# Input projections of an attention kernel, split into halves of the TensorE array's rows, with two-bank PSUM tiles

## Chip, cores and metric

One core of a Trainium2 chip runs the whole program. The metric is the device time of one execution in microseconds (us), the median of the runs shown. The profile is of one further execution on the same kernel.

The engines go by the profile's names: PE is TensorE, PEld its weight loads, DVE is VectorE, ACT is ScalarE, POOL is GpSimd, SP is SyncE, which issues most DMAs.

## What is computed

Two layers of multi-head attention with decomposed relative position biases, each on group-normalized input with a residual. There are 4 images of 32 x 32 positions (S = 1024) and 768 channels, 12 heads of 64 channels. Cut to what matters:

```
for layer in (0, 1):
    y = group_norm(x)                         # 32 groups
    q, k, v = y @ Wqkv (+ bias in layer 1)    # 12 heads, d = 64
    bias[h, w, kh, kw] = r_q . Rh[h - kh] + r_q . Rw[w - kw]
    scores = scale * q @ k.T + bias           # 1024 x 1024 for each head
    out = softmax(scores) @ v
    x = x + out @ Wproj + bproj
# layer 0: scale = 1/8, r_q = q.   layer 1: q is scaled twice, r_q = q / 8
```

All data are fp32.

## The kernel before

**Units of work.** A layer and an image together are one of 8 stages, called images 0 to 7 below. An image has 6 pairs of heads (`NP`), a pair has 8 blocks of 128 queries (`NT`). The main loop (from L517) runs over 48 x 8 = 384 units. In unit n of pair g it does, in this order on PE:

- what earlier units left over in the list `early`: position products (`positions`, 16 small matmul records on a tile `tp`) and loads
- the scores of the following unit (`scores`, L328): for two heads and two halves of the keys, 4 fp32 matmuls. Head 0 uses rows 0 to 63 of the array, head 1 rows 64 to 127, and they write different PSUM tiles
- a share of the projections (`take`): the input projections of the next pair (`project_in`, L222: q, k and v, two halves of 512 columns each, so 6 groups of 6 fp32 matmuls), then output projections of this or the last image (`project_out`, groups of 3 matmuls)
- in every second unit `weigh`: the product with the values for two blocks, 16 matmuls on halves of the array's columns (tile `av`)
- twice in a pair `turn_values`: transposes of v on PE (tile `vt`).

An fp32 matmul shows as two MATMUL records and two LDWEIGHTS records. In most pairs units 0 to 5 each hold one whole input group (q, q, k, k, v, v) and units 6 and 7 two output groups each. Pair 5 of an image takes output groups in units 0 and 1 first and the input groups in units 2 to 7. Pair 4 also carries the normalization of the next image (`norm`): its small matmuls `gm` and `gb` stand behind the first four input groups. In image 0 and at the end of image 7, where fewer output groups are there, groups reach across units.

**What the other engines do in a unit.** DVE makes the negated scores with their row minimum (L342, one instruction for each head), ACT the exponentials (L346), DVE the reciprocals (L350), POOL the weights (L353), DVE the 32 x 32 block transposes (L367). The weights then go through DRAM and come back as `pt`, four units later used by `weigh`. POOL also lays out the biases `sc` two units ahead (L323).

**PSUM.** [...]`ps_s` has 3 buffers of two banks, used by the scores and by `tp`. `ps_m` has 2 buffers of one bank, used by everything else on PE: `pj` (input projection), `o`, `av`, `vt`, `gm`, `gb`. A group on a `ps_m` buffer can start when the group before the last one has been evicted.

**Evictions of the input projections.** q goes through ACT with its scale (L247, L249), k and v through DVE (L251, L253). v is written in a strided order. When a q half is there, `positions` for it is put into `later` (or `early` for the first pair of an image) and so runs two (one) units later; `scores` of the next pair needs both halves of q and k; `turn_values` needs v.

**What sets the order.** PE runs in the program's order (a manual schedule). The other engines' instructions are put in an order by the compiler's scheduler, which then stands; each engine works through its own queue in that order. `early`, `later` and `late` are lists of steps for the next unit, for the one after it, and for the end of a unit.

The core of the two steps that the change touches:

```
            nc.tensor.matmul(
                t, lhsT=w[:, c, :], rhs=xn[c][:, cols],
                start=(c == 0), stop=(c == NC - 1),
            )
...
                nc.tensor.matmul(
                    ps[h][:, cols], lhsT=q[rows, n * P : (n + 1) * P], rhs=k[rows, cols],
                    start=True, stop=True,
                )
```

The first is the input projection, over all 128 rows. The second is the scores, where `rows` is one half.

Of the kernel before, what the change touches and what calls it, by code (L numbers as in the profile page):

```python
# [30 lines left out]
P = 128  # L32
# [16 lines left out]
def attention_blocks(ctx: ExitStack, tc: tile.TileContext, a: dict, out: bass.AP):  # L49
# [20 lines left out]
    ps_s = ctx.enter_context(tc.tile_pool(name="ps_s", bufs=3, space=PSUM))  # L70
# [74 lines left out]
    nc.gpsimd.tensor_scalar(bqkv[:, 0, :], bqkv[:, 0, :], SCALE * SCALE, None, ALU.mult)  # L145
# [22 lines left out]
    def group_mean(cols, name):  # L168
        t = ps_m.tile([P, HALF], FP, tag="m", name=f"gm_{name}")
        for c in range(NC):  # L170
            nc.tensor.matmul(
                t[0:NG, 0:1], lhsT=grp[:, c, :], rhs=cols(c), start=(c == 0), stop=(c == NC - 1)
            )
        return t[0:NG, 0:1]

    def to_channels(g, name):
        t = ps_m.tile([P, HALF], FP, tag="m", name=f"gb_{name}")
        for c in range(NC):
            nc.tensor.matmul(
                t[:, c : c + 1], lhsT=grpT[:, c * P : (c + 1) * P], rhs=g, start=True, stop=True  # L180
            )
        return t[:, 0:NC]
# [39 lines left out]
    def project_in(g, which, i):  # L222
# [11 lines left out]
        t = ps_m.tile([P, HALF], FP, tag="m", name=f"pj_{g}_{which}_{i}")  # L234
        for c in range(NC):
            nc.tensor.matmul(  # L236
                t, lhsT=w[:, c, :], rhs=xn[c][:, cols],
                start=(c == 0), stop=(c == NC - 1),
            )
            if c < NC - 1:  # L240
                yield True
        if which == 2:
            t = t.rearrange("p (y k j) -> p y k j", y=2, k=NT)
        bias = bqkv[:, which, pair : pair + 1]
        if which == 0:
            if l == 0:
                nc.scalar.activation(to, t, AF.Copy, scale=SCALE)  # L247
            else:
                nc.scalar.activation(to, t, AF.Identity, bias=bias, scale=SCALE * SCALE)  # L249
        elif l == 0:  # L250
            nc.vector.tensor_copy(to, t)  # L251
        else:
            nc.vector.tensor_scalar(to, t, bias, None, ALU.add)  # L253
        if which == 0:
            (later if pair else early).append(lambda: positions(g, i))
        if which == 2 and i == 1:
            late.extend([lambda: turn_values(g, 0), lambda: turn_values(g, 1)])
# [6 lines left out]
    def turn_values(g, i):  # L264


        if i == 0:
            v_of[g] = vpool.tile([P, NT, P], FP, tag="v", name=f"v_{g}")
        t = ps_m.tile([P, 4, P], FP, tag="m", name=f"vt_{g}_{i}")
        for j in range(4):  # L270
            at = 4 * i + j
            nc.tensor.transpose(t[:, j, :], qkv_of[g, 2][:, at * P : (at + 1) * P], ident)  # L272
        nc.scalar.copy(v_of[g][:, 4 * i : 4 * i + 4, :], t)  # L273

    def positions(g, i):
# [6 lines left out]
        ps = ps_s.tile([P, 2, 4, P], FP, tag="s", name=f"tp_{g}_{i}")  # L282
# [45 lines left out]
    def scores(g, n):  # L328
        q, k = qkv_of[g, 0], qkv_of[g, 1]
        ps = [ps_s.tile([P, S], FP, tag="s", name=f"s_{g}_{n}_{h}") for h in range(2)]  # L330
        for i in range(2):
            cols = slice(i * HALF, (i + 1) * HALF)
            for h in range(2):
                rows = slice(h * D, (h + 1) * D)
                nc.tensor.matmul(  # L335
                    ps[h][:, cols], lhsT=q[rows, n * P : (n + 1) * P], rhs=k[rows, cols],
                    start=True, stop=True,
                )
        st = small.tile([P, 3, 2], FP, tag="sm", name=f"sm_{g}_{n}")
        for h in range(2):  # L340
            sc = sc_of[g, n, h].rearrange("p y x -> p (y x)")
            nc.vector.tensor_tensor_reduce(  # L342
                out=sc, in0=ps[h], in1=sc, scale=-1.0, scalar=BIG, op0=ALU.add, op1=ALU.min,
# [37 lines left out]
    def weigh(g, quarter):  # L381
        if quarter == 0:
            attn_of[g] = apool.tile([P, S], FP, tag="attn", name=f"attn_{g}")
        av = ps_m.tile([P, HALF], FP, tag="m", name=f"av_{g}_{quarter}")[:, : 2 * P]
# [45 lines left out]
    def project_out(im, p, o, i):  # L430
# [7 lines left out]
        t = ps_m.tile([P, HALF], FP, tag="m", name=f"o_{im}_{p}_{o}_{i}")  # L438
# [168 lines left out]
```

## Time and profile before

| | us |
|---|---|
| median of 3 runs | 3851.63 (3844.91 to 3860.61) |
| profiled execution, its own time | 3855.63 |
| its span, first to last instruction | 3853.9 |
| PE busy | 3716.4 (96%) |
| DVE busy | 2353.1 (61%) |
| POOL busy | 2316.3 (60%) |
| ACT busy | 1148.9 (30%) |
| granted TensorE clock, mean | 0.987 |

Busy times add up the durations of an engine's instructions where they do not overlap. A row of the costliest groups gives line, engine, operation, what it writes and reads, its count, then busy time and the mean ns of one, then the idle time of the engine just before and what ended it. In the timeline each row has start and duration in us, and in brackets the idle time of that engine before it.

### The profile page before, as it was taken

What the parts mean: (1) busy time and instruction counts of PE and PEld (TensorE: products, weight loads), DVE (VectorE), ACT (ScalarE), POOL (GpSimd) and SP (SyncE); (2) the same over time, 40 slices, a digit from 0 to 9 for tenths busy, and PEclk for the clock granted to TensorE, in tenths of its full rate; (3) what the DMA queues carried; (4) which work ended last, traced back from release to release, by engine and by line L of the source; (5) the groups of instructions that cost most, each with busy time, mean ns of one, the idle gap of its engine ahead of it and who ended that gap; (6) DMA issues with size and microseconds to landing.
All of it is one profiled execution on the core that took longest, in us unless ns stands there. A gap on an engine that the chain in (4) does not pass through costs nothing.

```text
span 3853.9 us, 45565 instructions
## 1 busy us (share of the span) xinstructions
PE 3716.4 (96%) x16128; PEld 1716.4 (45%) x16128; DVE 2353.1 (61%) x3520; ACT 1148.9 (30%) x1848; POOL 2316.3 (60%) x1555
## 2 busy tenths in 40 slices
PE   8899999999999999999999999999999999999998
PEld 3444444444444444444444444444444444444443
DVE  4566656656566665665656656666566665656663
ACT  1233232222332323333323332233323332233330
POOL 4666556655565656666566655666566665666671
PEclk9999999999999999999999999999999999999999
DMA  5778778887788887887878888888788887988877
GB/s 179 266 274 302 276 272 294 295 291 277 279 293 283 307 289 264 305 301 277 312 254 298 292 279 295 289 298 297 255 318 290 291 278 278 314 284 282 293 271 269
DMA packets 620820, 1094.73 MB, mean 284 GB/s; under 512 B 235056, under 2 KB 295728, under 8 KB 571440
## 3 DMA queue, kind: packets, MB, share of 16 engines
q1 hardware_dynamic: 569904, 1041.49, 77.9%
q10 hardware_dynamic: 50688, 50.34, 3.8%
q8 instruction: 127, 2.08, 0.2%
q14 instruction: 101, 0.83, 0.1%
HBM read 588.36 MB, written 503.32 MB: 283 GB/s over the span
## 4 chain that ended last, share of the span: by engine, by line
PE 77%; DMA 8%; DVE 5%; ACT 3%; issue 3%; POOL 2%; SPq 1%; DVEq 0%; ACTq 0%; POOLq 0%
PE pj L236 32%; PE av L388 16%; PE s L335 15%; PE o L440 11%; PE tp L287 2%; ACT sc L346 2%; DVE tb L367 2%; DMA tdr<-t 2%; POOL sc L353 2%; DVE sc L342 1%; SPq L313 1%; DMA xs<-in_x 1%; DMA td<-tb 1%; PE vt L272 1%; DMA w<-in_wqkv 1%
## 5 line engine op out<-in xcount | busy, mean ns | idle before, releaser
L323 POOL TENSOR_TENSOR sc<-rel 128x1024 f32<-128x1024 f32 x768 | 1456.3, 1916 | 270.3 <-DMA rel<-tdr 140.9
L236 PE MATMUL pj<-xn,w 128*128 128x512 f32 x3456 | 1579.0, 606 | 31.5 <-DVE k L251 12.7
L353 POOL TENSOR_SCALAR sc<-sc,sm 128x1024 f32<-128x1024 f32 x768 | 854.9, 1126 | 1205.0 <-DVE sm L350 1200.1
L346 ACT ACTIVATE sc<-sc,sm 128x1024 f32<-128x1024 f32 x768 | 878.5, 1144 | 1863.7 <-DVE sm L342 1793.1
L367 DVE STREAM_TRANSPOSE tb<-sc 128x1024 f32<-128x1024 f32 x768 | 921.0, 1227 | 464.9 <-POOL sc L353 462.6
L342 DVE CUSTOM_DVE_ANT_0 sc<-s,sc 128x1024 f32<-128x1024 f32 x768 | 906.1, 1216 | 303.3 <-PE s L335 303.2
L236 PEld LDWEIGHTS pj<-xn,w 128*128 128x128 f32 x3456 | 638.4, 191 | 951.1 <-issue 884.0
L388 PE MATMUL av<-pt,v 128*64 128x256 f32 x6144 | 730.6, 392 | 61.3 <-DVE g L202 22.9
L335 PE MATMUL s<-k,q 64*128 64x512 f32 x3072 | 764.1, 610 | 4.1 <-DVE sm L342 4.0
L388 PEld LDWEIGHTS av<-pt,v 128*64 128x64 f32 x6144 | 435.8, 141 | 406.9 <-issue 72.4
L440 PE MATMUL o<-attn,wo 128*128 128x512 f32 x1152 | 524.4, 605 | 5.0 <-DVE res L449 4.2
L335 PEld LDWEIGHTS s<-k,q 64*128 64x128 f32 x3072 | 268.2, 186 | 318.5 <-issue 306.4
L440 PEld LDWEIGHTS o<-attn,wo 128*128 128x128 f32 x1152 | 211.5, 190 | 310.4 <-issue 291.2
L350 DVE RECIPROCAL sm<-sm 128x2 f32<-128x2 f32 x384 | 63.6, 166 | 442.1 <-ACT sc L346 442.1
L292 ACT COPY t<-tp 128x1024 f32<-128x1024 f32 x96 | 97.1, 1011 | 292.9 <-PE tp L287 291.2
L393 DVE COPY attn<-av 128x256 f32<-128x256 f32 x192 | 78.5, 409 | 120.5 <-PE av L388 120.0
L273 ACT COPY v<-vt 128x512 f32<-128x512 f32 x96 | 56.1, 585 | 319.3 <-PE vt L272 319.1
L346 ACT ACTIVATION_READ_ACCUMULATOR sc<-sc,sm 128x1 f32 x768 | 143.1, 186 | 0.0
L287 PE MATMUL tp<-tab,q 64*128 64x128 f32 x1536 | 111.6, 285 | 6.6 <-ACT q L249 3.1
L287 PEld LDWEIGHTS tp<-tab,q 64*128 64x128 f32 x1536 | 93.2, 187 | 52.9 <-issue 32.7
L447 DVE SCALAR_TENSOR_TENSOR res<-o,bo,res 128x512 f32<-128x512 f32 x96 | 70.1, 730 | 16.5 <-PE o L440 15.0
L449 DVE TENSOR_TENSOR res<-o,res 128x512 f32<-128x512 f32 x96 | 64.6, 674 | 22.3 <-PE o L440 12.3
(47 smaller groups left out, 646.1 us busy)
## 6 DMA issues: line engine op xcount, KB each, us to landing
td<-tb SPq DMA_DIRECT2D x384, 1024.0 KB, 5.9
pt<-td SPq DMA_DIRECT2D x384, 1024.0 KB, 7.4
w<-in_wqkv SPq DMA_DIRECT2D x144, 384.0 KB, 7.5
tdr<-t ACTq DMA_DIRECT2D x96, 512.0 KB, 6.8
rel<-tdr SPq DMA_DIRECT2D x768, 32.0 KB, 2.0
part<-res SPq DMA_DIRECT2D x96, 256.0 KB, 6.5
res<-part SPq DMA_DIRECT2D x96, 256.0 KB, 4.6
wo<-in_wo SPq DMA_DIRECT2D x84, 192.0 KB, 6.0
```

Of the source, the lines that this page charges most:

```text
L236: nc.tensor.matmul(t, lhsT=w[:, c, :], rhs=xn[c][:, cols], start=(c == 0), stop=(c == NC - 1),)
L287: nc.tensor.matmul(ps[:, h, j, :], lhsT=q[rows, at * P : (at + 1) * P], rhs=tabs[l][rows, :], start=True, stop=True,)
L292: nc.scalar.copy(t, ps.rearrange("p h j r -> p j h r"))
L323: nc.gpsimd.tensor_tensor(sc, rel[:, h, 0, n, :].unsqueeze(2).to_broadcast([P, HW, HW]), rel[:, h, 1, n, :].unsqueeze(1).to_broadcast([P, ...
L335: nc.tensor.matmul(ps[h][:, cols], lhsT=q[rows, n * P : (n + 1) * P], rhs=k[rows, cols], start=True, stop=True,)
L342: nc.vector.tensor_tensor_reduce(out=sc, in0=ps[h], in1=sc, scale=-1.0, scalar=BIG, op0=ALU.add, op1=ALU.min, accum_out=st[:, 0, h : h + 1],)
L346: nc.scalar.activation(sc, sc, AF.Exp, bias=st[:, 0, h : h + 1], scale=-1.0, accum_out=st[:, 1, h : h + 1],)
L353: nc.gpsimd.tensor_scalar(sc, sc, st[:, 2, h : h + 1], 1.0, ALU.mult, ALU.mult)
L367: nc.vector.transpose(tb[:, :, j, :], sc_of[g, n, h])
L388: nc.tensor.matmul(av[rows, :], lhsT=v_of[g][:, k, rows], rhs=pt_of[g, quarter, h][:, :, k, :], start=(k == 0), stop=(k == NT - 1),)
L393: nc.vector.tensor_copy(attn_of[g][:, at : at + 2 * P].rearrange("p (n r i) -> p r n i", n=2, r=4), av.rearrange("p (r n i) -> p r n i", n ...
L440: nc.tensor.matmul(t, lhsT=w[:, c - c0, :], rhs=attn_of[im * NP + c][:, cols], start=(c == c0), stop=(c == c1 - 1),)
```

## The change

```
-    ps_s = ctx.enter_context(tc.tile_pool(name="ps_s", bufs=3, space=PSUM))
+    ps_s = ctx.enter_context(tc.tile_pool(name="ps_s", bufs=2, space=PSUM))
     ps_m = ctx.enter_context(tc.tile_pool(name="ps_m", bufs=2, space=PSUM))
...
-    nc.gpsimd.tensor_scalar(bqkv[:, 0, :], bqkv[:, 0, :], SCALE * SCALE, None, ALU.mult)
...
-        t = ps_m.tile([P, HALF], FP, tag="m", name=f"pj_{g}_{which}_{i}")
+        t = ps_m.tile([P, 2, HALF], FP, tag="m", name=f"pj_{g}_{which}_{i}")
         for c in range(NC):
-            nc.tensor.matmul(
-                t, lhsT=w[:, c, :], rhs=xn[c][:, cols],
-                start=(c == 0), stop=(c == NC - 1),
-            )
+            for a in range(2):
+                rows = slice(a * D, (a + 1) * D)
+                nc.tensor.matmul(
+                    t[:, a, :], lhsT=w[rows, c, :], rhs=xn[c][rows, cols],
+                    start=(c == 0), stop=(c == NC - 1),
+                )
             if c < NC - 1:
                 yield True
+        t = [t[:, a, :] for a in range(2)]
         if which == 2:
-            t = t.rearrange("p (y k j) -> p y k j", y=2, k=NT)
-        bias = bqkv[:, which, pair : pair + 1]
-        if which == 0:
-            if l == 0:
-                nc.scalar.activation(to, t, AF.Copy, scale=SCALE)
-            else:
-                nc.scalar.activation(to, t, AF.Identity, bias=bias, scale=SCALE * SCALE)
-        elif l == 0:
-            nc.vector.tensor_copy(to, t)
+            t = [x.rearrange("p (y k j) -> p y k j", y=2, k=NT) for x in t]
+        if l == 0:
+            nc.scalar.copy(to, t[0])
         else:
-            nc.vector.tensor_scalar(to, t, bias, None, ALU.add)
+            nc.scalar.activation(to, t[0], AF.Identity, bias=bqkv[:, which, pair : pair + 1])
+        nc.vector.tensor_tensor(to, t[1], to, ALU.add)
...
-            late.extend([lambda: turn_values(g, 0), lambda: turn_values(g, 1)])
+            late.append(lambda: turn_values(g))
...
+    def turn_values(g):
+        v_of[g] = vpool.tile([P, NT, P], FP, tag="v", name=f"v_{g}")
+        t = ps_m.tile([P, NT, P], FP, tag="m", name=f"vt_{g}")
+        for k in range(NT):
+            nc.tensor.transpose(t[:, k, :], qkv_of[g, 2][:, k * P : (k + 1) * P], ident)
+        nc.scalar.copy(v_of[g], t)
...
-        ps = ps_s.tile([P, 2, 4, P], FP, tag="s", name=f"tp_{g}_{i}")
+        ps = ps_m.tile([P, 2, 4, P], FP, tag="m", name=f"tp_{g}_{i}")
...
+        scale = SCALE if g // NP < B else SCALE * SCALE
...
-                out=sc, in0=ps[h], in1=sc, scale=-1.0, scalar=BIG, op0=ALU.add, op1=ALU.min,
+                out=sc, in0=ps[h], in1=sc, scale=-scale, scalar=BIG, op0=ALU.add, op1=ALU.min,
```

Each fp32 matmul of an input projection becomes two, one for channels 0 to 63 of a chunk and one for 64 to 127. They write two banks of one tile. ACT copies the first bank to SBUF (with the bias in layer 1) and DVE then adds the second bank to it, for q, k and v alike. The scale of q moves into the scale of L342. All tiles of `ps_m` now have two banks, still in 2 buffers; `ps_s` goes from 3 buffers to 2, and `tp` moves from `ps_s` to `ps_m`. `turn_values` runs once in a pair over 8 blocks, in place of twice over 4, with one copy of 1024 elements in place of two of 512.

More of the change, by code (lines that the diff above doesn't have):

```diff
@@ L168, in group_mean @@
     def group_mean(cols, name):
-        t = ps_m.tile([P, HALF], FP, tag="m", name=f"gm_{name}")
+        t = ps_m.tile([P, S], FP, tag="m", name=f"gm_{name}")
         for c in range(NC):
@@ L176, in to_channels @@
     def to_channels(g, name):
-        t = ps_m.tile([P, HALF], FP, tag="m", name=f"gb_{name}")
+        t = ps_m.tile([P, S], FP, tag="m", name=f"gb_{name}")
         for c in range(NC):
@@ L262, in project_in @@
         yield True
[L264 to L273, printed above, removed]
+    def turn_values(g):
[4 more added lines that the diff above has]
+        nc.scalar.copy(v_of[g], t)
     def positions(g, i):
@@ L383, in weigh @@
             attn_of[g] = apool.tile([P, S], FP, tag="attn", name=f"attn_{g}")
-        av = ps_m.tile([P, HALF], FP, tag="m", name=f"av_{g}_{quarter}")[:, : 2 * P]
+        av = ps_m.tile([P, S], FP, tag="m", name=f"av_{g}_{quarter}")[:, : 2 * P]
         for k in range(NT):
@@ L437, in project_out @@
         w, res = wo_of[im, p, o], res_of[im, p, o, i]
-        t = ps_m.tile([P, HALF], FP, tag="m", name=f"o_{im}_{p}_{o}_{i}")
+        t = ps_m.tile([P, S], FP, tag="m", name=f"o_{im}_{p}_{o}_{i}")[:, :HALF]
         for c in range(c0, c1):
```

## Prediction

> **What bounds the kernel now.** I read the busy times, then the costliest groups, then the timeline of two units (numbers 2 and 3 of a pair) and the table of windows for whole pairs.
>
> ```profile
> PE 3716.4 (96%) x16128; PEld 1716.4 (45%) x16128; DVE 2353.1 (61%) x3520; ACT 1148.9 (30%) x1848; POOL 2316.3 (60%) x1555
> ...
> L236 PE MATMUL pj<-xn,w 128*128 128x512 f32 x3456 | 1579.0, 606 | 31.5 <-DVE k L251 12.7
> L335 PE MATMUL s<-k,q 64*128 64x512 f32 x3072 | 764.1, 610 | 4.1 <-DVE sm L342 4.0
> L449 DVE TENSOR_TENSOR res<-o,res 128x512 f32<-128x512 f32 x96 | 64.6, 674 | 22.3 <-PE o L440 12.3
> ```
>
> PE is the bound. The second and third row say more: 3456 full-array records take 1579 us, 457 ns for each; 3072 half-array records of the same 512 columns take 764, so 497 for each two. Two halves run side by side. The fourth row is an add from PSUM and SBUF as the change makes.
>
> ```profile
> 1050.00 1.89 PE L335 MATMUL s<-k,q 64*128 64x512 f32 x8
> 1051.81 0.30 PEld L236 LDWEIGHTS pj<-xn,w 128*128 128x128 f32 x2 [0.76 <-issue]
> 1051.91 1.23 DVE L342 CUSTOM_DVE_ANT_0 sc<-s,sc 128x1024 f32<-128x1024 f32 x1 [2.34 <-PE s L335]
> 1052.35 0.19 PEld L236 LDWEIGHTS pj<-xn,w 128*128 128x128 f32 x1 [0.24 <-issue]
> 1052.78 0.19 PEld L236 LDWEIGHTS pj<-xn,w 128*128 128x128 f32 x1 [0.24 <-issue]
> 1057.08 2.37 DVE L367 STREAM_TRANSPOSE tb<-sc 128x1024 f32<-128x1024 f32 x2 [1.25 <-POOL sc L353]
> 1057.16 0.30 PEld L335 LDWEIGHTS s<-k,q 64*128 64x128 f32 x4 [0.76 <-issue]
> 1059.08 0.30 PEld L236 LDWEIGHTS pj<-xn,w 128*128 128x128 f32 x2 [0.76 <-issue]
> 1059.38 0.65 DVE L251 COPY k<-pj 128x512 f32<-128x512 f32 x1
> 1059.95 1.21 DVE L342 CUSTOM_DVE_ANT_0 sc<-s,sc 128x1024 f32<-128x1024 f32 x1
> ```
>
> Inside a group a weight load comes every 0.43 us (1052.35, 1052.78), so 12 records should take 5.15 us; from 1051.81 to 1057.16 they take 5.35. The next scores, 4 pairs or 1.72, take 1.92 (1057.16 to 1059.08). Each passage between full and half array costs 0.20 us: the weight load comes 0.76 after the last one, in place of 0.24, because it isn't laid under the matmuls before. From `tp` to the scores, both on halves, the trace shows no such time (2 to 3 ns over the plain spacing).
>
> ```profile
> 2107.00:2182.30 75.30, 75.30 (x329) 34.58 (x329) 48.85 (x75) 23.62 (x38) 48.02 (x32) 1.00 0.86 294
> 2257.60:2347.30 89.70, 84.11 (x386) 40.31 (x385) 55.61 (x82) 26.47 (x41) 48.95 (x33) 0.98 0.79 283
> 2347.30:2423.80 76.50, 72.22 (x319) 32.82 (x318) 46.74 (x71) 23.02 (x37) 46.47 (x32) 1.00 0.88 300
> ```
>
> The first row is an ordinary pair (pair 2 of image 4): PE never stops in 75.3 us. The next are pairs 4 and 5: 5.6 and 4.3 us of PE waiting.
>
> [...]a k eviction whose matmuls ended at 1057.2 started at 1059.38, behind two transposes.
>
> **The change part by part.** The sum is made against the profiled execution (3855.63 us, 4.0 above the median).
>
> *Matmuls.* 1728 fp32 matmuls become 1728 pairs. By the scores' spacing (429 ns for a pair of records, 429 for a full record) their time is unchanged. The two halves of the scores already write two banks; that accumulating over six chunks costs nothing more is shown by `av`, whose pairs accumulate eight times at 216 ns for 256 columns. I take 0.
>
> *Passages.* In the order of the matmuls I count 292 from scores to `pj`, 90 from `pj` to scores, 35 from `pj` to `tp`. All become half to half: 417 x 0.20 = **83 us less**, or 9 x 0.20 = 1.8 in an ordinary pair. `pj` to `av` remains a change of form; one transpose step fewer saves 8 more passages to `tp`, 1.6, which I leave aside.
>
> *Eviction.* ACT takes 0.6 (row q<-pj, 595 ns in layer 0), then DVE adds, 0.67 for q and k; for v, strided, its copy took 1.07 and I take 1.1, bounds 0.67 and 1.6. ACT (30%) has long done its exponentials when a group ends, so its copy hides. DVE gets 96 additional instructions (q), 64 us, and the k and v ones change little. What counts is when a `ps_m` buffer comes free. From the timeline, with 0 at a unit's first L342: second transpose ends at 7.5 (1059.45 - 1051.91); a group ends at 5.3; the add is ready at 6.0, when the first transpose is on DVE. The second is then ready too and stands first in the program, as for k above, so the add runs to 8.15. q's buffer used to be free at 5.9.
>
> *Who waits for that.*
> (a) Ordinary pair: k's first half (unit 2) now takes the buffer of q's second half, since `tp` stands between on the other. Unit 1 has no `av`: with the passage gone its group starts 0.2 ahead of the L342 that is my 0, so PE is back after 5.15 + `tp` 0.9 + scores 1.72 - 0.2 = 7.6; the buffer comes at 8.15, and the signal and a weight load that is not laid under anything add some 0.2: 0.7 us. There are 27 such pairs (0 to 3 of images 1 to 6, 0 to 2 of image 7): **+19**.
> (b) Pair 4, 7 times. After q's first half and `gm`, `av` needs q's buffer. Before, it started at 2271.44, 5.7 after the first L342 of its unit (2265.77); the add ends at 8.2: +2.6. After q's second half and `gb`, `tp` needs that buffer: it started 6.7 after (2283.73 against 2277.06), now at 8.3: +1.5. DVE catches up in these stalls, so about 1.0 of its lag at the next scores goes. 3.1 x 7 = **+22**.
> (c) Pair 5, 7 times: `tp` follows q's second half at once and needs its data. It waited 0.9 before; now until 8.2 in place of 6.1: 2.1 x 7 = **+15**.
> (d) Seven pairs with few output groups (0 to 3 of image 0, 3 to 5 of image 7) follow DVE's chain more than PE: two units are there 2 x 1.72 + 9 x 0.86 + `av` 3.5 = 14.7 on PE, and 2 x 7.5 + evictions on DVE. Their 1.8 isn't harvested, and q adds 2 x 0.6: 3.1 x 7 = **+22**.
>
> *Other edits at nothing.* Two score buffers in place of three: scores need both L342 of the unit before, done 2.4 after it starts, while PE is back after 7 or 10.5; DVE would have to lag by 4 us. `vt` in one piece: one copy of 1.0 in place of two of 0.59, hidden under the next scores. The scale on POOL ran once. No DMA is added; `tp`'s store waits for the same copy, in pair 5 some 2 us later, well ahead of its use a pair on.
>
> *Sum.* -83 + 19 + 22 + 15 + 22 = -5: 3851 in the profile, **3847 us** on the median's footing. v's add at 1.6 or 0.67 adds up to 15 or takes 10.
>
> **The rivals.**
> *The adds slip in between the two transposes.* For it: output evictions do so in unit 6 (a residual add starts at 1084.73 between transposes at 1083.56 and 1085.30). Against it: k doesn't, with an earlier ready time. The buffer is then free 1.15 sooner: (a) vanishes, (b) and (c) lose about 3.5 of 5.2 a stage (24 us). 3847 - 19 - 24 = **3804**.
> *Slower: DVE's queue behind one buffer.* In (a) the next unit's first L342 (1.2 us) stands ahead of q's add on DVE, so k waits 1.9 in place of 0.7. For it: DVE is already 0.8 late after a unit without `av` (L342 at 1059.95, scores ended at 1059.15), and unit 1 now has such an eviction too. Against it: by the dependences the add is ready a scores' length earlier. 34 pairs x 1.2 = 41: **3888**. It decides from 1.8 us of waits in a pair, where the passages' gain is used up.
> *The halves don't run side by side*, so the change doesn't do what it says: 1728 x 0.86 = 1486 more, 5330. The score rows speak against it.
>
> **How the numbers follow.** A measurement of this kernel can tell some 0.5%, 19 us, from no change. Forecast (within 19 us) 0.46; gain kept 0.27; slower by the queue 0.25; not side by side 0.02. Range: from the first rival less some microseconds of a cheaper v add, 3800, to the second, 3888, and a little of the dearer v add: 3892. 0.46 lies within 3830 to 3866.
>
> **What would show it.** Right: the weight load of `pj` after scores comes 0.24, not 0.76, after the last one; `pj` pairs every 0.43; an ordinary pair lasts 74.2; in its unit 2 `pj` waits for DVE q some 0.7; pair 4 grows by 1 or 2 us; PE's idle time names DVE q at `av` and `tp`. Wrong: ordinary pairs at 73.5 (first rival), at 75.5 or more (second), or 0.86 between pairs of records (third).

## The result, and the profile after

| | before | after |
|---|---|---|
| median of the runs side by side | 3848.4 us (3844.9 to 3860.6, 4 runs) | 4035.9 us (4029.6 to 4042.8, 4 runs) |
| ratio | 1 | 1.0482, 95% interval 1.045 to 1.0513 |
| span of the profiled execution | 3853.9 us | 4030.2 us |
| granted TensorE clock, mean | 0.987 | 0.962 |

The changed kernel is 4.8% slower; 3847 with a range of 3800 to 3892 had been forecast. On the page of the changed kernel, the busy times and four of the costliest groups, and below them the last of these rows as it was before:

```profile
PE 3696.3 (92%) x19584; PEld 1778.8 (44%) x19584; DVE 2397.5 (59%) x3616; ACT 1314.8 (33%) x1992; POOL 2307.3 (57%) x1554
...
L241 PE MATMUL pj<-xn,w 64*128 64x512 f32 x6912 | 1555.0, 595 | 46.3 <-DVE q L254 37.7
...
L387 PE MATMUL av<-pt,v 128*64 128x256 f32 x6144 | 734.0, 393 | 81.1 <-DVE v L254 31.8
L333 PE MATMUL s<-k,q 64*128 64x512 f32 x3072 | 778.2, 620 | 9.6 <-DVE sm L341 9.5
...
L439 PE MATMUL o<-attn,wo 128*128 128x512 f32 x1152 | 540.2, 619 | 74.6 <-DVE v L254 69.4
```

```profile
L440 PE MATMUL o<-attn,wo 128*128 128x512 f32 x1152 | 524.4, 605 | 5.0 <-DVE res L449 4.2
```

PE's busy time fell by 20 us while the span grew by 176: PE does not work longer, it waits. 6912 half-array records take 1555 us where 3456 full ones took 1579, so the halves do run side by side. The last column says who waits: before, the output rows waited 5.0 us in all; now they wait 69 us for DVE's add of v (L254), and `av` another 32. Those rows are not the ones that the change rewrote.

Two units of an ordinary pair in the timeline of the changed kernel (some of the PE, PEld and DVE lines of pair 2 of image 4, units 1 and 2):

```profile
2243.04 5.32 PE L241 MATMUL pj<-xn,w 64*128 64x512 f32 x24
2243.24 1.22 DVE L341 CUSTOM_DVE_ANT_0 sc<-s,sc 128x1024 f32<-128x1024 f32 x1 [0.81 <-PE s L333]
2243.47 0.19 PEld L241 LDWEIGHTS pj<-xn,w 64*128 64x128 f32 x2 [0.24 <-issue]
2248.41 2.37 DVE L366 STREAM_TRANSPOSE tb<-sc 128x1024 f32<-128x1024 f32 x2 [1.25 <-POOL sc L352]
2249.08 1.89 PE L333 MATMUL s<-k,q 64*128 64x512 f32 x8
2250.70 0.65 DVE L254 TENSOR_TENSOR q<-pj,q 128x512 f32<-128x512 f32 x1
2251.41 0.30 PEld L241 LDWEIGHTS pj<-xn,w 64*128 64x128 f32 x4 [1.27 <-DVE q L254]
2251.41 1.13 PE L241 MATMUL pj<-xn,w 64*128 64x512 f32 x4 [0.44 <-DVE q L254]
```

The weight loads of `pj` come 0.24 us after the load before, with no 0.76 at the passage, and 24 records take 5.15 us to `tp` (2243.04 to 2248.19, the start of the `tp` records). The q add stands behind both transposes and ends 8.1 after the unit's first L341, and k's first half starts after it: 0.60 us later than the matmul spacing allows. This part went as forecast.

The windows of pairs 2, 4 and 5 of image 4 in the changed kernel (columns: start and end, length, then busy time and instructions of PE, PEld, DVE, ACT, POOL; then PE's clock, DMA share, GB/s):

```profile
2225.30:2299.86 74.56, 73.89 (x401) 35.48 (x401) 49.69 (x76) 27.45 (x41) 47.74 (x32) 1.00 0.88 300
2374.10:2474.95 100.85, 84.27 (x450) 41.06 (x449) 55.43 (x84) 30.04 (x44) 47.94 (x32) 0.92 0.71 252
2474.95:2551.60 76.65, 73.33 (x382) 34.67 (x384) 47.95 (x72) 24.91 (x39) 46.60 (x32) 1.00 0.86 301
```

The first is the ordinary pair: 74.6, of which 0.3 is a wait elsewhere; the pairs next to it take 74.28 and 74.27. Pair 5: 76.7 against 76.5. Pair 4: 100.9 against 89.7, with PE's clock at 0.92. Where it is lost is seen in the DVE timeline of that pair (three more normalizations, L215, at the dots):

```profile
2448.81 2.37 DVE L366 STREAM_TRANSPOSE tb<-sc 128x1024 f32<-128x1024 f32 x2 [1.25 <-POOL sc L352]
2457.56 0.81 DVE L215 TENSOR_SCALAR xn<-xn,mean,rstd 128x1024 f32<-128x1024 f32 x1 [6.38 <-DMA xn<-mid]
...
2462.11 1.05 DVE L254 TENSOR_TENSOR v<-pj,v 128x512 f32<-128x512 f32 x1
2463.06 0.81 DVE L215 TENSOR_SCALAR xn<-xn,mean,rstd 128x1024 f32<-128x1024 f32 x1
2463.79 1.22 DVE L341 CUSTOM_DVE_ANT_0 sc<-s,sc 128x1024 f32<-128x1024 f32 x1
```

and in PE's timeline beside it:

```profile
2448.60 1.88 PE L333 MATMUL s<-k,q 64*128 64x512 f32 x8
2450.41 2.84 PE L439 MATMUL o<-attn,wo 128*128 128x512 f32 x6
2463.21 5.17 PE L439 MATMUL o<-attn,wo 128*128 128x512 f32 x6 [9.96 <-DVE v L254]
2468.31 3.67 PE L387 MATMUL av<-pt,v 128*64 128x256 f32 x32
```

The matmuls of the v group ended at 2448.6. Its add is queued on DVE behind four normalizations of the next image's input, which wait for their load until 2457.56; DVE stands idle for 6.4 us with the v add and the score reductions (L341) behind it. The reductions come some 13.3 us after their scores ended (2463.79 against 2450.5). In the kernel before, the v eviction and the reductions stood first:

```profile
2330.92 1.10 DVE L253 TENSOR_SCALAR v<-pj,bqkv 128x512 f32<-128x512 f32 x1
2331.88 1.20 DVE L342 CUSTOM_DVE_ANT_0 sc<-s,sc 128x1024 f32<-128x1024 f32 x1
...
2336.24 0.81 DVE L212 TENSOR_SCALAR xn<-xn,mean,rstd 128x1024 f32<-128x1024 f32 x1 [2.00 <-DMA xn<-mid]
```

In the seven pairs 4 together PE is idle for 115.0 us, for 44.6 before. 69.4 of it are the waits of `o` for v's add; at the same place `av` waited 19.9 for output evictions before.

The second thing to see is 5.17 against 2.84 us for the same six records: after the stall PE starts a record every 0.853 us instead of every 0.429, with a granted clock of 0.53 (2463.2 to 2468.3).

By part of the run, as differences of the profiled spans (start: until the first L341; pairs: from one pair's first score reduction to the next). The second column spreads the prediction's terms over the same parts, with the passages that each holds in the order of the matmuls: 9 in an ordinary pair, 7 in pair 4, 8 in pair 5, 66 in image 0 and the end. (Its terms add up to -6.4 with their decimals, -5 as the prediction rounds them.)

```
part                                   forecast   after - before, us
start                                    -0.4        +26.2
image 0, pairs 0 to 3                    +3.6        +43.7
image 7, pairs 3 and 4                   +1.8        +33.3
pair 4, seven times                     +11.9        +60.3
pair 5, seven times                      +3.5        +10.7
images 1 and 2, pairs 1 to 3             -6.6        +18.5
images 3 to 7, ordinary pairs, 14       -15.4        -14.7
pair 0 and the tail                      -4.8         -1.7
sum                                      -6.4       +176.2
```

The compiler leaves a fixed order of DVE's queue in each kernel. Below are its start and its part in pair 4, read from the traces of the kernels before and after and of three experiments. First line of each: evictions (q, k, v) and statistics of a loaded half of a later image (.) ahead of the first score reduction. Second line: pair 4 around the normalizations (tb transpose, sc reduction, xn normalization, v its eviction or add, res output eviction, rcp reciprocal; small steps left out).

```
before                .....kkv.v.
                      tb tb v sc sc xn res rcp xn tb res tb xn
layout alone          .....kkv.v.
                      tb tb v sc sc xn res rcp xn tb res tb xn
full rows, two steps  q...q...kkv.v.
                      tb tb v sc sc xn res rcp xn tb res tb xn
halves, one step      .........k.k...v...v
                      sc sc rcp tb tb xn xn xn v xn xn sc sc xn res
after                 ..q....q...k.k...v...v
                      sc sc rcp tb tb xn xn xn xn v xn sc sc xn res
```

### The profile page after: what moved, and what is told of

It reads as the page before. It is cut to its first block, busy times and chain, and to the rows that moved or that the text cites. A ratio compares the mean times of both kernels' runs of the same rounds, so it can differ in the third digit from the quotient of the medians.

```text
span 4030.2 us, 52794 instructions
## 1 busy us (share of the span) xinstructions
PE 3696.3 (92%) x19584; PEld 1778.8 (44%) x19584; DVE 2397.5 (59%) x3616; ACT 1314.8 (33%) x1992; POOL 2307.3 (57%) x1554
## 4 chain that ended last, share of the span: by engine, by line
PE 58%; DVE 11%; DMA 9%; ACT 8%; issue 7%; POOL 4%; SPq 1%; ACTq 0%; DVEq 0%; POOLq 0%
PE pj L241 19%; PE av L387 14%; PE s L333 12%; PE o L439 9%; ACT sc L345 8%; DVE tb L366 4%; POOL sc L352 4%; DMA xs<-in_x 3%; DVE sc L341 2%; PE tp L285 2%; DMA tdr<-t 2%; PE vt L270 1%; SPq L311 1%; DMA xn<-mid 1%; DVE q L254 1%
## 5 line engine op out<-in xcount | busy, mean ns | idle before, releaser
L241 PE MATMUL pj<-xn,w 64*128 64x512 f32 x6912 | 1555.0, 595 | 46.3 <-DVE q L254 37.7
L341 DVE CUSTOM_DVE_ANT_0 sc<-s,sc 128x1024 f32<-128x1024 f32 x768 | 907.3, 1216 | 365.4 <-PE s L333 365.3
L241 PEld LDWEIGHTS pj<-xn,w 64*128 64x128 f32 x6912 | 672.8, 189 | 891.5 <-issue 780.9
L333 PE MATMUL s<-k,q 64*128 64x512 f32 x3072 | 778.2, 620 | 9.6 <-DVE sm L341 9.5
L439 PE MATMUL o<-attn,wo 128*128 128x512 f32 x1152 | 540.2, 619 | 74.6 <-DVE v L254 69.4
L333 PEld LDWEIGHTS s<-k,q 64*128 64x128 f32 x3072 | 283.9, 192 | 330.9 <-issue 298.3
L285 PEld LDWEIGHTS tp<-tab,q 64*128 64x128 f32 x1536 | 101.5, 198 | 111.0 <-DVE q L254 45.2
L271 ACT COPY v<-vt 128x1024 f32<-128x1024 f32 x48 | 48.6, 1012 | 244.7 <-PE vt L270 244.7
L254 DVE TENSOR_TENSOR v<-pj,v 128x512 f32<-128x512 f32 x96 | 101.7, 1059 | 0.0
L270 PE MATMUL vt<-ident,v 128*128 128x128 f32 x384 | 56.4, 294 | 35.0 <-DVE v L254 15.5
```

Source lines behind the costliest of these rows:

```text
L241: nc.tensor.matmul(t[:, a, :], lhsT=w[rows, c, :], rhs=xn[c][rows, cols], start=(c == 0), stop=(c == NC - 1),)
L254: nc.vector.tensor_tensor(to, t[1], to, ALU.add)
L285: nc.tensor.matmul(ps[:, h, j, :], lhsT=q[rows, at * P : (at + 1) * P], rhs=tabs[l][rows, :], start=True, stop=True,)
L333: nc.tensor.matmul(ps[h][:, cols], lhsT=q[rows, n * P : (n + 1) * P], rhs=k[rows, cols], start=True, stop=True,)
L341: nc.vector.tensor_tensor_reduce(out=sc, in0=ps[h], in1=sc, scale=-scale, scalar=BIG, op0=ALU.add, op1=ALU.min, accum_out=st[:, 0, h : h + 1],
L439: nc.tensor.matmul(t, lhsT=w[:, c - c0, :], rhs=attn_of[im * NP + c][:, cols], start=(c == c0), stop=(c == c1 - 1),)
```

## The experiments

The theory from the traces: the matmuls are as forecast, and the loss comes from the order of DVE's queue, which the compiler fixed differently once the input projections were halves. The rivals: the second eviction step costs by itself; the halves cost on PE; the other layout (banks, buffers, `tp` in `ps_m`) costs. The differences in the table are of profiled spans against the kernel before (3853.9), by the parts of above; the ratios are of medians, with the 95% interval. A profiled execution lay up to 15 us from the median of its kernel (e8 15 above, e11 and e12 12 below), so a few us in one part decide nothing.

```
run                     ratio  [interval]           span   start   im.0    end   pair4  pair5  im.1-2  im.3-7   rest
after                   1.0482 [1.0450, 1.0513]  +176.2   26.2   43.7   33.3    60.3   10.7    18.5   -14.7   -1.7
e1  halves, one step    1.0312 [1.0288, 1.0337]  +113.2   25.5   19.3   18.9    56.3   13.1     3.8   -23.1   -0.6
e2  full, two steps     1.0295 [1.0274, 1.0316]  +108.5    4.9   16.3   12.2    30.6   20.6    17.4     1.7    4.6
e3  after, DVE by hand  1.0127 [1.0104, 1.0149]   +39.1    1.8   13.4   18.8   -40.0   48.7   -14.2     7.5    3.0
e4  before, DVE by hand 1.0217 [1.0190, 1.0243]   +81.4   -1.7  -11.2    5.1   -12.9   37.6     3.6    48.8   12.1
e5  layout alone        1.0081 [1.0053, 1.0109]   +17.8   -0.5   -4.0   -0.7     0.1    7.6     6.9     0.0    8.3
e6  after, pipelined    0.9961 [0.9950, 0.9971]    -8.2    2.0    3.7   13.6   -70.5   93.4   -18.6   -15.2  -16.6
e7  before, pipelined   0.9866 [0.9844, 0.9887]   -59.8   -1.2  -18.4   -2.8   -75.1   56.2   -17.1     0.0   -1.4
e8  after, adds first   1.0265 [1.0246, 1.0284]  +111.9    2.3   49.3   33.3    53.2   11.7   -22.0   -15.0   -0.8
e9  e1, evictions first 1.0156 [1.0133, 1.0179]   +52.6    0.0   21.2   20.1    61.5    1.4   -24.2   -25.0   -2.4
e10 after, whole groups 1.0272 [1.0253, 1.0291]   +98.9   22.9   -6.9    1.0    64.9   14.9    20.0   -14.2   -3.7
e11 e6 and whole groups 0.9867 [0.9846, 0.9888]   -67.7    1.7  -27.4    0.3   -74.3   87.1   -19.1   -21.1  -14.9
e12 before, v late      1.0073 [1.0050, 1.0095]   +17.7   -2.1   -1.0   -0.1     9.3   10.0    -2.8     0.0    4.4
e13 after, all repairs  1.0007 [0.9994, 1.0021]    +2.9    2.8   -7.3    0.3   -18.1   66.0   -22.8   -15.0   -2.9
e14 e7 and whole groups 0.9802 [0.9774, 0.9831]   -72.0   -1.0  -28.1   -5.7   -75.1   55.6   -17.1     0.0   -0.6
e15 e11, wo by ACT      0.9778 [0.9752, 0.9803]   -82.7    3.1  -22.7    1.4   -74.3   62.8   -15.8   -23.8  -13.4
e16 before, all repairs 1.0025 [1.0013, 1.0036]    -0.4   -0.9   -6.1    1.0   -41.5   49.0   -13.2     0.0   11.3
e17 e14, wo by ACT      0.9742 [0.9724, 0.9760]  -108.0   -1.5  -27.8   -5.7   -75.1   23.2   -17.1     0.0   -3.9
e18 before, DVE late    1.0088 [1.0067, 1.0110]   +27.3   -0.2   -1.4   -0.6    32.4    2.4    -1.9     0.0   -3.4
```

**Which part of the change (e1, e2, e5).** Each takes the changed kernel and puts one part back. e1 keeps the halves and evicts the first bank alone by the engines of before; it leaves out half of each input projection's sum, though all matmuls still run. e2 keeps the two steps and computes with full rows: ACT writes zero times the bank (plus bias), DVE adds the bank. e5 keeps the layout alone. The edits, shortened (layer 0 only):

```
e1  -        nc.vector.tensor_tensor(to, t[1], to, ALU.add)
    +        t = t[:, 0, :]
    +        if which == 0: nc.scalar.copy(to, t)
    +        else: nc.vector.tensor_copy(to, t)
e2  +            nc.tensor.matmul(t[:, 0, :], lhsT=w[:, c, :], rhs=xn[c][:, cols], ...)
    +            nc.scalar.activation(to, t, AF.Copy, scale=0.0)
    +        nc.vector.tensor_tensor(to, t, to, ALU.add)
e5  the matmul of e2 with the eviction of e1
```

> Half-array matmuls as in the change, but the first of the two banks alone is evicted, in one step and by the engines of before (q by ACT, k and v by DVE); the second bank is left out, so half of every input projection's sum is missing. Order theory (the scheduler counts the two halves one after the other, takes an input group for 10 us in place of 5, and so puts DVE's evictions behind work that comes later on the chip): DVE's queue has the changed order here too, with the k eviction behind 9 statistics at the start and the last v eviction behind the normalization in pair 4; ordinary pairs 73.5 us (passages gone, no wait for q), but the start, image 0, the end and pair 4 stay longer than before: 3880 to 3970 in all. Eviction theory (the copy and the add in a row hold the buffers too long): with one step the loss is gone and the passages' gain is left, 3760 to 3790.

> Full-array matmuls as before in one bank, but with the eviction in two steps (ACT writes zero times the bank plus the bias, DVE adds the bank), and the PSUM layout of the change. Order theory: DVE's order is nearly that of before, so only the waits that were counted ahead (ordinary pairs some 0.3 to 0.7 us, pair 4 some 3, pair 5 some 2) are added to the time of before: 3890 to 3930. Eviction theory: the loss of the change and the passages come together, 4050 to 4120.

> The PSUM layout of the change (two score buffers, two-bank tiles elsewhere, the position products among them, values turned in one step) with full-array matmuls and the evictions of before. Order theory, in which the two-step eviction costs its 110 us by itself through waits on the buffers: within 15 of before, 3840 to 3870. Rival: of the 110 us that the kernel with full rows and two steps lost, the fewer buffers are the greater part: 3910 to 3960, and the halves and the second step matter less than they seemed.

The layout costs 0.8%. The halves alone lose 25 us at the start and 56 in pair 4, as the changed kernel does, with no second step; the two steps alone lose 5 and 31 there. In ordinary pairs the halves gain 1.8 us each (75.35 to 73.56) and the changed kernel 1.1, so the q add costs 0.7. The queue orders above divide in the same way: both kernels with halves have the late order, all three with full rows the order of before in pair 4. So the halves move the order, and the second step is not needed for it. Why the compiler does so isn't shown: it fits a compiler that counts the two halves one after the other, 10.3 us for a group in place of 5.15, and therefore finds other work ready ahead of each eviction; this is inferred from the orders alone.

Neither theory has all of it, though. The second step with full rows costs 91 us over e5 (108.5 against 17.8), and e2 at 3966 us is slower than the order theory allowed (3890 to 3930). In the seven pairs 4, where the order around the normalizations is that of before, it is 31. So the second step costs by itself as well: somewhat more than the 78 of terms (a) to (d), and about what the passages give.

**DVE's order by hand (e3, e4, e6, e7).** e3 and e4 give DVE the program's order in both kernels; e6 and e7 another one, written out: the reductions of the next unit, the two transposes with the first output eviction between, reciprocal, normalization, then the group's eviction.

```
-    with tc.manual_schedule(engines={mybir.EngineType.PE}):
+    with tc.manual_schedule(engines={mybir.EngineType.PE, mybir.EngineType.DVE}):
...
+            turn(g, n, (0,))
+            take(todo, first)
+            turn(g, n, (1,))
+            weights(*units[at + 1])
+            for c in cs: apply(c)
+            take(todo, share - first)
```

(Shortened; the lines with + from `turn` on are in e6 and e7 only.)

> The change whole, with DVE's instructions too held in the program's order in place of the scheduler's. Order theory: no add stands behind statistics or normalization that wait for loads, ordinary pairs at 73.5 or less, start and image 0 as before or shorter: 3740 to 3800. Eviction theory: the adds still follow the copies, the waits stay: 3950 to 4040. A third possibility is that the program's order brings waits of its own (the reciprocal ahead of the transposes), which the next kernel, without the change, would share.

> The kernel before with DVE held in the program's order; the control for the run ahead of it. Order theory: it loses what waits it had on DVE, 60 to 100 us less than before, 3750 to 3800, and the change is then worth 0 to 60 on top of it. Eviction theory: the same time here, and the change on top of it is 150 slower.

> The change with DVE held in an order written for it: reductions of the next unit, then the transposes of this one while ACT makes the exponentials, the first output eviction between them, then the reciprocal, the normalization, then the adds. Order theory: an add starts when it is ready, some 6 us after the unit's first reduction in place of 7.5; ordinary pairs at 73.5 or a little less, waits in pairs 4 and 5, at the start and the ends small: 3660 to 3760, below the kernel before. Eviction theory: two steps in a row hold the buffers whatever the order, 3850 to 3950.

> The kernel before with the same order of DVE. Order theory: ordinary pairs at 75.3, as PE never stops in them, the waits elsewhere smaller: 3740 to 3800, so 60 to 80 above the change in the same order, which is what the passages are worth. Eviction theory: here the order brings as much, and the change in the same order isn't faster.

With DVE's order fixed by hand the changed kernel no longer has its 26 us at the start and its 60 in pair 4, in both orders: 1.0482 falls to 1.0127 and 0.9961. What the change is worth depends on the order, though: in the program's order it is ahead of its control (1.0127 against 1.0217), in the other one behind (0.9961 against 0.9866), which is what the rival theory of the eviction had said of e7. Three of the four times were not those of the order theory: e3 (3903 us) and e6 (3837) were slower than it allowed, and e4 (3935) came out slower than the kernel before in place of faster. Only e7 (3798) lies in its range. Image 0 and the end stay worse than the control in both orders.

**One place at a time, order left to the compiler (e8, e9, e10).** e8 (changed kernel) and e9 (the halves of e1, with the same part left out) hold statistics and normalizations behind the latest input eviction that DVE makes. e10 gives each unit a whole input group where groups reached across units.

```
e8, e9
+    def behind_add(f):
+        with tc.issue_after(last_add[0]):
+            f()
...
+        later.append(lambda: behind_add(lambda: stats(im, c, i, x)))
...
+                    behind_add(lambda: apply(2 * ((n + 1) % NT) + c))
e10
-            take(todo, -(-left(todo) // (NT - n)))
+            take(todo, max(-(-left(todo) // (NT - n)), NC if todo and todo[0][1] == NC else 0))
```

> The change, with one thing held fast in DVE's queue: the statistics of loaded images and the normalization stand behind the latest add ahead of them in the program. Order theory: of the 26 us lost ahead of the first pair nearly all goes, and 15 to 20 in images 0 to 2 where adds stood behind statistics; in pair 4 the last v add no longer waits for the next image's load, but reductions still stand behind the normalization, so 2 to 5 of some 9 a stage go; the waits of groups that reach across units stay. 3940 to 3990. If the order of these few instructions isn't what matters: 4020 to 4040.

> The same hold on DVE's queue in the kernel with half-array matmuls and a one-step eviction of the first bank (half of each input projection's sum is left out). Order theory: 3974 less 25 at the start, 10 to 15 in images 0 to 2 and 15 to 30 in pair 4: 3900 to 3925. If half-array matmuls cost by something else than the order: 3960 to 3980.

> The change, with input groups held to one unit each in image 0 and at the end of image 7 as they are elsewhere (6 matmul pairs in each of units 0 to 5). If the loss there comes from groups that end in mid-unit, so that their copy stands behind ACT's exponentials and a third tile wants a buffer: pairs 0 to 2 of image 0 and 3 and 4 of image 7, which lost 10 to 19 each, come within 3 of before: 3965 to 3985 in all. If it comes from the order of DVE there alone: no more than 20 less, 4015 to 4035.

e8 empties the start (26.2 to 2.3) and turns images 1 and 2 from +18.5 to -22.0: that part was adds behind statistics, which wait for their loads (at the start of the changed kernel one every 3.4 us or so, with 1.7 to 7.2 us of DVE idle before each). Pair 4 stays, in e8 and e9 alike, where 2 to 5 us a stage less had been expected, though v is now ahead of the normalizations: in e9 `av` waits 62.4 us in all for output evictions that stand behind them instead. e10 empties image 0 and the end (77.0 to -5.9) and hardly anything else. One such wait is in the changed kernel's timeline of ACT, DVE and PE in image 0, one fence each (some lines), the last fence being PE at the same place before:

```profile
246.91 1.15 ACT L345 ACTIVATE sc<-sc,sm 128x1024 f32<-128x1024 f32 x1 [5.04 <-DVE sm L341]
248.05 1.15 ACT L345 ACTIVATE sc<-sc,sm 128x1024 f32<-128x1024 f32 x1
249.20 1.05 ACT L251 COPY v<-pj 128x512 f32<-128x512 f32 x1
```

```profile
250.74 1.25 DVE L366 STREAM_TRANSPOSE tb<-sc 128x1024 f32<-128x1024 f32 x1 [1.25 <-POOL sc L352]
251.91 1.03 DVE L254 TENSOR_TENSOR v<-pj,v 128x512 f32<-128x512 f32 x1
```

```profile
243.10 3.60 PE L241 MATMUL pj<-xn,w 64*128 64x512 f32 x16
252.99 5.19 PE L387 MATMUL av<-pt,v 128*64 128x256 f32 x32 [6.29 <-DVE v L254]
```

```profile
204.41 6.37 PE L388 MATMUL av<-pt,v 128*64 128x256 f32 x32 [3.97 <-DVE v L251]
```

A group that ends in mid-unit, at 246.7, meets ACT as it starts on the two exponentials. The copy waits for them until 249.20, the add then for a transpose, and `av` for the add: 6.3 us, in place of 4.0 before. The copy is not the whole of the 77: in e1, where DVE alone evicts k and v, 38 are lost in the same pairs. e10, whose groups end with their units, takes both away.

**Is the order enough, without the change (e12, e18)?** Both take the kernel before. e12 puts the second v eviction of pair 4 behind four normalizations (and so lets their load start some 2.5 us earlier); e18 puts the two following reductions behind them too, with the load where it was. The edit is that of e18; e12 has the same lines, without the hold on the reductions, at the place of the eviction itself.

```
e18
+        def evict_v():
+            load_x(im + 1)
+            for c in range(4):
+                last_norm[0] = norm_of[im + 1](c).ins
+            with tc.issue_after(last_norm[0]):
+                nc.vector.tensor_copy(to, t)
...
+            with tc.issue_after(last_norm[0]):
                 nc.vector.tensor_tensor_reduce(...)
```

> The kernel before, with its own matmuls and single evictions; only the place of one DVE instruction in each of seven images is changed: the second v eviction of pair 4 stands behind the first four normalizations of the next image's input (their load is issued when that v group has ended), as it stands in the changed kernel. If the order of DVE's queue is what costs in pair 4, the outputs behind it wait some 8 us for the buffer as they do in the changed kernel: pair 4 longer by 6 to 10 us in each image, 45 to 70 in all, some 3910 us. If the second eviction step or the matmuls on halves are needed for the loss, DVE makes up for one late eviction and the run stays within 15 us of the kernel before.

> The kernel before with its own matmuls and single evictions; in pair 4 of seven images not only the second v eviction but also the two score reductions of the next unit stand on DVE behind the first four normalizations, and the load for them is not issued earlier than in the kernel before. That is what stands there in the changed kernel. If the loss in pair 4 is DVE standing before a load with the reductions behind it, pair 4 grows by 4 to 8 us in each image, 28 to 56 in all, near 3890 us. If the matmuls on halves or the second step are needed, pair 4 grows by no more than the 9 us in all that the v eviction alone gave.

e12 lies between the numbers of its two theories: v was evicted 8 us later, the second output group waited, yet pair 4 grew by 9.3 in all, in place of 45 or more. The theory that the place of the v eviction alone makes the loss falls. In e12 the reductions still ran 3.6 us after their scores. `o` now waited 37.3 us in the seven pairs, but the 19.9 that `av` had waited behind it were gone. e18 has the reductions behind the load as well. Its DVE timeline in image 4:

```profile
2341.34 2.37 DVE L380 STREAM_TRANSPOSE tb<-sc 128x1024 f32<-128x1024 f32 x2 [1.25 <-POOL sc L366]
2349.25 0.81 DVE L212 TENSOR_SCALAR xn<-xn,mean,rstd 128x1024 f32<-128x1024 f32 x1 [5.54 <-DMA xn<-mid]
...
2357.69 1.15 DVE L255 TENSOR_SCALAR v<-pj,bqkv 128x512 f32<-128x512 f32 x1
2358.68 1.22 DVE L355 CUSTOM_DVE_ANT_0 sc<-s,sc 128x1024 f32<-128x1024 f32 x1
```

DVE stands 5.5 us before the load, the reductions come 15 us after their scores, and pair 4 grows by 32.4, with the matmuls and evictions of before: about half of the 60.3. It is not the changed kernel's order to the letter, since output evictions slip in among the normalizations here; PE waits 44.6 us at this place, 69.4 in the changed kernel.

**All repairs, order left to the compiler (e13, e16).** Statistics behind evictions, whole groups, and the normalizations at the end of their units behind the latest eviction, output eviction and reduction; e13 in the changed kernel, e16 in the one before.

```
+            if not end and (pair, n) in ((NP - 2, 7), (NP - 1, 0), (NP - 1, 1)):
+                with tc.issue_after(last_red[0]), tc.issue_after(last_out[0]):
+                    for c in range(2):
+                        behind_add(lambda: apply(2 * ((n + 1) % NT) + c))
```

> The changed kernel with all three repairs that leave the order to the compiler: statistics of loaded halves behind the latest add, whole input groups in each unit, and the normalization moved from the start to the end of its units and held behind the latest add, output eviction and score reduction. If the loss was the order of DVE's queue, all three places lose their excess: start from +26 to about +2, image 0 and end from +77 to about -5, pair 4 from +60 to between -15 and +20, images 1 and 2 about -20, so 3810 to 3850 us and level with the kernel before or ahead of it. If the wait in pair 4 belongs to the two-step eviction itself, pair 4 keeps +50 or more and the run ends at 3870 or above.

> The kernel before with the same three repairs as the last compiler-ordered run of the changed kernel (3857 us, ratio 1.0007): the control for it. In ordinary pairs the change is worth 1.1 us each there, and about 20 more in images 1 and 2; in pairs 4 and 5 its second eviction step costs 3.1 and 2.1 us an image by the prediction, 36 us. If the change is worth about nothing once the order is the same, this run lies between 3840 and 3865 us, ratio 0.996 to 1.003. If the second step costs more than the passages give, it is faster than that; if the passages win, slower.

The changed kernel comes from 1.0482 to 1.0007, 3857 us and a little above what was expected. Start, image 0, end and images 1 and 2 are as expected, pair 4 a little shorter; pair 5 is not, +66: the normalizations are now there, and the control has +49 too. The two kernels stand level (1.0007 and 1.0025, the intervals overlap). Between them pair 4 differs by +23.4, pair 5 by +16.9 and ordinary pairs by -1.1 each. PE's waits there differ in sum by 20.9 and 16.6, close to terms (b) and (c), 22 and 15. The passages saved in these pairs, 9.8 and 11.2 us, don't show: PE spent 18 and 21 us more of its busy time at half clock, which is 9 and 10 us lost if half the clock means half the rate (an estimate from the clock in the two traces, and from the 0.853 us in place of 0.429 that the changed kernel showed at 0.53).

**The better order with whole groups, and the queue for the output weights (e11, e14, e15, e17).** e11 and e14 are e6 and e7 with the groups of e10 and the normalizations three by three at the end of units 0 and 1 of pair 5. Both then wait in pair 5 for the output weights `wo` (82 us in e11, 48 in e14), whose loads stand on SP's queue behind stores (in e11 one issued at 2279.05, behind two stores that SP began at 2275.06); e15 and e17 load them from ACT's queue.

```
-                nc.sync.dma_start(
+                nc.scalar.dma_start(
                     out=w[:, : c1 - c0, :],
```

> The change in the written order of DVE, now with the normalization behind each unit's work in units 0 and 1 of pair 5 (it stood ahead of output evictions and waited for the image's load there), and with whole input groups in each unit. Order theory: pair 5 loses most of the 13 us by which it exceeded before, image 0 and the end some 20 in all: 3700 to 3760, which is below the kernel before and below 3797. Otherwise 3820 to 3840 as without these two edits.

> The control for the last hand-ordered run of the changed kernel (3801 us, 67.7 us of span gained): the kernel before with the same hand-written DVE order, whole groups and normalizations by threes. The changed kernel's own gain in ordinary pairs is 1.1 us each, 14 pairs, and 12 more each in pair 0 and in images 1 and 2, so if the change is worth what its passages give, this run is 10 to 40 us slower, 3810 to 3840. If the second eviction step takes back as much as the passages give, the two are equal within 8 us.

> The hand-ordered changed kernel (3801 us) with the loads of the output weights issued by ACT's queue in place of SP's. In pair 5 the outputs and the scores behind them waited 4 to 9 us for these loads, which stand on SP behind stores that wait for evictions. If SP's order is what costs there, pair 5 falls from +87 to +20 to +50 and the time to 3735 to 3770. If the transfers themselves are late (the DMA engines full, or the weights' buffer not free), pair 5 stays within 10 us of +87.

> The control for the fastest run of the changed kernel (3772 us, ratio 0.9778): the kernel before in the same hand-written order with the output weights on ACT's queue. The wait for these weights was 48 us of the kernel before in that order and 82 of the changed one, and moving them gave the changed kernel some 15 us of span. If the weights' queue was what held the changed kernel back, the two are now equal or the changed one ahead: ratio 0.977 to 0.985. If the second eviction step still costs, this run is faster, below 0.975.

Pair 5 falls by 24 (87.1 to 62.8) in the changed kernel, between its two theories, and by 32 (55.6 to 23.2) in the control: SP's order was part of it. Most of what stays in e15 is the next load on SP, that of the residual (e15, DVE):

```profile
2286.10 0.75 DVE L450 SCALAR_TENSOR_TENSOR res<-o,bo,res 128x512 f32<-128x512 f32 x1 [4.47 <-DMA res<-mid]
```

In pair 5 PE waits 41 us for the output evictions that follow this load, 13 in e17.

e11 (3801 us) lies between its two expectations. e14 was expected to be equal at best; it is faster, by 4 us of span and by 0.65% in the ratios. e17 came out below 0.975, which had been named as the sign that the second step still costs. In this order the change loses in both comparisons: 0.9867 against 0.9802, and 0.9778 against 0.9742, where the intervals overlap a little. The best kernel of the study is e17, the matmuls and evictions of before in an order of DVE written by hand: 3751.6 us, 2.6% faster than before. Its busy line has PE at 98% of the span:

```profile
PE 3678.1 (98%) x16128; PEld 1700.6 (45%) x16128; DVE 2339.8 (62%) x3520; ACT 1150.4 (31%) x1848; POOL 2309.4 (62%) x1555
```

## Why the prediction was wrong

The sum of -5 us was nearly right for the terms in it, with the exception of (d), and the terms that made the result were not in it.

- **Matmuls and passages: right.** `pj` pairs come every 0.429 us; the passage of 0.20 is gone; ordinary pairs gain 1.8 without the q add (e1), nine passages of 0.20.
- **(a) right:** 0.60 us of wait in place of 0.7, an ordinary pair 74.27 in place of 74.2.
- **(b) and (c) right in size.** Apart from the 69.4 for v, PE waits 45.6 us in the seven pairs 4, against 24.7 before: 20.9 more, (b) said 22. In pair 5 `tp` waits 23.3 us for q's add, before 5.2 for q: 18.1 more, (c) said 15 (the waits of `pj` for v fell by 13 there at the same time).
- **Eviction, the failed step.** "The second is then ready too and stands first in the program": I took DVE's order from the trace of before, here and for all that stands around the evictions, though it is the compiler that fixes it, with the changed matmuls in its count. In ordinary pairs that order held. At the start, in images 1 and 2 and in pair 4 it did not. It cost 24 us at the start (26.2 to 2.3 in e8) and 40 in images 1 and 2 (18.5 to -22.0 in e8, part of which the kernel before was paying already). In pair 4 PE waits 69.4 for v's add where it waited 19.9 before, 49.5 more; e18 brings 32.4 us with the order alone. None of the three has a term in the sum, since the trace of before doesn't show them.
- **"ACT (30%) has long done its exponentials when a group ends, so its copy hides": failed in the pairs of (d).** It held where a group ends with its unit: q's copy in the ordinary pair started at 2248.40, 0.2 us after the last records of its group. In (d), groups end in mid-unit; the copy of the fence above waited for both exponentials, until 2.5 us after its group's end. For six of its seven pairs (d) and the passages made +5.4; it measured +77.0, and e10 takes all of it away. e1 loses 38 there with k and v evicted in one step, so about half of the 77 is there without the copy.
- **The rivals.** The one on the slow side had DVE's queue behind a buffer, but in the ordinary pair, by one reduction of 1.2 us. It was the right engine with the wrong instruction: a normalization that waited 6.4 us for its load. The range ended at 3892 for that reason.
- **The clock.** No term allowed for what PE loses after a long stall (below). By the clock in the traces PE stood at half clock for 305 us of the changed kernel and for 103 before, in part while it waited. What this cost in all was not separated from the waits.

What stays open: why the compiler moves the other work ahead of the evictions (inferred, as said at e1), and how the cost of the second step alone, 91 us in e2 against e5, comes about outside pairs 4 and 5. Whether one step could take both banks was not shown either.

## What to carry to other kernels

An order that a compiler fixed is part of what a change changes: where only one engine is ordered by hand, compare the compiled queues of the others before and after, and look for instructions that wait for a load and now stand ahead of evictions or reductions. The price of an eviction in two steps over two engines differed here with the point in the unit: 0.60 us of wait in an ordinary pair, and 6.3 us at a group that ended in mid-unit, 4.0 there before; ask it of each place where a group can end, and not of the ordinary one alone. To judge a change of matmuls, give both kernels the same order first: here the change took between 0.9% off the time (e3 against e4) and 1.0% more (e6 against e7) by the order chosen, and the order by hand with its queue for the weights took 2.6% off without the change (e17).

## What the runs showed of the hardware

- After a PE stall of 9.96 us (changed kernel, image 4, 2463.21) six fp32 records of 512 columns started 1.015 us apart at first and then, four times, 0.853 us apart, in place of 0.429; the clock granted in these 5.1 us was 0.53. In the 3.7 us that followed it was 1.00, and the next tile, `av`, took its usual 3.67 us. The mean granted clock of the whole execution fell from 0.987 to 0.962.
- In the changed kernel, with v's strided order, the copy of 128x512 took ACT a median of 1125 to 1229 ns, against 585 to 687 for q and k, and DVE's add 1060 against 652.
- Accumulating pairs of half-array matmuls into two banks ran at the rate of the full array, 0.429 us a pair of records over all six chunks.
